# A decoder kernel: queries and keys written to DRAM as they are, and stacks gathered from them by many small DMAs

## The chip, the cores and the metric

The kernel runs on one core of a Trainium2 chip. A core has a matrix engine (TensorE, PE in the profile), a vector engine (VectorE, DVE), a scalar engine (ScalarE, ACT), GpSimd (POOL), and SyncE (SP), whose queue issues nearly all of this kernel's DMAs. Sixteen DMA engines move the data between DRAM and the on-chip memory of 128 partitions. The metric is the time of one execution on the device in microseconds (us), the median of several runs; lower is better.

## The reference

Input is x of shape 32 x 128 x 128 (batch, position, feature) and a context of the same shape. Two decoder layers follow each other, each part followed by a residual sum and a layer norm. Layer 0: an RWKV mixer, a block with self-attention, cross-attention and a feed-forward net, and a mixture of eight experts. Layer 1: a self-attention with rotary positions, a cross-attention, and a mixture of experts with capacity. The change touches the two attentions of layer 1. Both have 16 heads of dimension 8:

```
q = split_heads(x @ Wq + bq); k = split_heads(x @ Wk + bk); v = split_heads(x @ Wv + bv)
q = _rope(q); k = _rope(k)                                  # self-attention only
scores = einsum('bhqd,bhkd->bhqk', q, k) / sqrt(8)
probs  = softmax(scores)                                    # self-attention
attn   = silu(where(mask == 0, -1e9, scores * 8**-0.5))     # cross-attention, in place of the softmax
out    = einsum('bhqk,bhkd->bhqd', probs or attn, v) ... @ Wo
```

## The kernel before, in words

The 32 sequences are worked in eight groups of four (G = 4, GT = 512 columns). Each layer part is cut into units, eight for a group, and `place` puts the steps of a unit at unit numbers: the self-attention's steps by the table L6, the cross-attention's by L7. `pipeline` sorts all steps by that number and calls them in order, so that steps of neighbouring groups and parts lie between each other; a scheduler then fixes each engine's instruction order by priority and readiness. On the chip every engine runs its own list in order and waits on semaphores. SP's list is such a list too: a DMA that waits for something holds up all DMAs behind it.

In both attentions of layer 1 the score products have only 8 rows for each head. To use the matrix engine's rows, and to keep nearly float32 accuracy with bfloat16 products, a query or key is split into three bfloat16 parts (`parts3`, on POOL, four instructions each for q and k, lines 739 to 742). A score is the sum of six products of such parts, and the six blocks of 8 rows lie one under another in a "stack": row blocks 0 to 2 hold part pairs (q1,k3), (q2,k2), (q3,k1), blocks 3 and 4 the pairs (q1,k2), (q2,k1), block 5 the pair (q1,k1). The stack's two planes z = 0 and z = 1 hold q and k. Even heads use partitions 0 to 63, odd heads 64 to 127; a stack covers two of the four sequences (256 of the 512 columns).

[...] `spill` (lines 763 to 766) writes the parts into a scratch tensor `d_st` that already has the stack's row order; a part that stands in several products is written several times: one DMA of 768 KB and three of 256 KB. Rows 48 to 63 of each half come from a constant, written at the start into each of three scratch tensors (line 750): zeros, and ones in two rows of plane 1. `stack` (line 777) then reads a stack with two DMAs of 512 KB, one for each half of the partitions, in 512-byte pieces. `take(h)` calls it for columns half h = 0 and 1. Stacks lie in buffers with the tag `big` (five buffers, shared with other uses), or, for h = 0 of the self-attention from the third group on, in a weight buffer `w8`.

In the self-attention a first round of products (`cross(j, 0)`) serves only to find each row's maximum (`smax`, line 903). `mrow` turns the maxima, `mwrite` (line 916) writes them to DRAM in two bfloat16 parts, and `mread` (line 922) reads them into rows 48 and 49 of plane 0, opposite the ones, so that the second round (`cross(j, 1)`, then the exponential, line 930) subtracts the maximum inside the product. The cross-attention has no maximum and one round (`probs`, products added to a mask written by line 1060). A round is eight products of 64 rows each, pairwise on the two halves of the partitions, issued by `block` (lines 164 and 169).

Line 177 loads a group's x and line 186 stores it, line 514 loads the context and line 1022 the mask.

Of the kernel before, what the change touches and what calls it, by code (L numbers as in the profile page):

```python
# [11 lines left out]
BF = mybir.dt.bfloat16  # L12
# [11 lines left out]
GT = G * 128  # L24
# [45 lines left out]
class Net:  # L70
# [673 lines left out]
    def scratch(self, k):  # L744

        if self.dst is None:
            self.dst = []
            for i in range(3):
                d = self.dp.tile([64, 2, 8, 2, GT], BF, name=f"d_st{i}")
                self.nc.sync.dma_start(out=d[48:64], in_=self.a["pad_bf"])  # L750
                self.dst.append(d)
        return self.dst[k % 3]

    def parts(self):
# [2 lines left out]

    def spill(self, k, p):

        dma = self.nc.sync.dma_start  # L760
        d = self.scratch(k)
        rows = lambda lo, n: d[lo * 8:(lo + n) * 8].rearrange("(a d) r q z t -> (d r q) a z t", d=8)
        dma(out=rows(0, 3), in_=p)
        for z in range(2):
            dma(out=rows(3, 2)[:, :, z, :], in_=p[:, z:z + 2, z, :])
        dma(out=rows(5, 1)[:, 0], in_=p.rearrange("p a z t -> p (a z) t")[:, 0:6:5, :])
        return d

    def stack(self, d, h, slab=False):

        if slab:
            s = self.wp.tile([128, 4128], BF, name="w8", tag="w8", bufs=W8)
            s = s[:, 0:8 * GT].rearrange("p (q z t) -> p q z t", q=8, z=2)
        else:
            s = self.t("stack", [8, 2, GT // 2], BF)
        for par in range(2):
            self.nc.sync.dma_start(out=s[par * 64:par * 64 + 64], in_=d[:, par, :, :, h * 256:h * 256 + 256])
        return s

    def pad9(self):  # L780
# [61 lines left out]
    def att_units(self, g, getw, done):  # L842
        nc, sm = self.nc, self.sm
        w = Later(getw)
        st = {}
# [28 lines left out]
            st["d"] = self.spill(g, st.pop("p"))  # L874

        def take(h):
            st["s", h] = self.stack(st["d"], h, g > 1 and h == 0)

        def vproj(b):
            st["v", b] = self.v9proj(g, b, st["xh"], st["xl"], w["w"][0][:, 512:640], w["w"][1][:, 512:640], w["bv"])  # L880
# [1 line left out]
        def cross(j, l):  # L882

            b, pq = j // 2, j % 2
            t = slice(b % 2 * 128, b % 2 * 128 + 128)
            sk = st["s", b // 2]
            s = [self.pst("cross1" if l else "cross0") for _ in range(2)]
            calls = []
            for k in range(4):
                for par in range(2):  # L890
                    p = slice(par * 64, par * 64 + 64)
                    calls.append((s[par][:, k * 128:(k + 1) * 128], sk[p, pq * 4 + k, l, t],
                                  sk[p, pq * 4 + k, 1 - l, t], dict(start=True, stop=True)))
            self.block(calls)
            return s
# [76 lines left out]
        for j in range(8):  # L972
            h, odd = j // 4, j % 2
# [36 lines left out]
    def xat_units(self, g, getw, done):  # L1010
        nc = self.nc
        w = Later(getw)
        st = {}
# [41 lines left out]
        def probs(j):  # L1055
            b, pq = j // 2, j % 2
            t = slice(b % 2 * 128, b % 2 * 128 + 128)
            s = [self.pst("silu1" if j % 2 else "silu0") for _ in range(2)]
            for par in range(2):
                nc.tensor.matmul(out=s[par], lhsT=self.identb,  # L1060
                                 rhs=st["m"][:, b, :].unsqueeze(1).to_broadcast([128, 4, 128]), start=True, stop=False)
            calls = []
            for k in range(4):
                for par in range(2):
                    r = slice(par * 64, par * 64 + 64)
                    calls.append((s[par][:, k * 128:(k + 1) * 128], st["s", b // 2][r, pq * 4 + k, 1, t],
                                  st["s", b // 2][r, pq * 4 + k, 0, t], dict(start=False, stop=k == 3)))
            self.block(calls)
            ps = []
            for par in range(2):  # L1070
                p = self.t("xp")
                nc.scalar.activation(p, s[par], AF.Tanh, scale=0.5 * 8 ** -0.5)
                st["last", j] = nc.vector.scalar_tensor_tensor(p, p, 1.0, s[par], ALU.add, ALU.mult)
                ps.append(p)
            st["p", j] = ps
# [377 lines left out]
def prep(i):  # L1453
    c = np.ascontiguousarray
    f = np.float32
    pairs = lambda w: c(w.reshape(8, 128, 128).transpose(1, 0, 2).reshape(128, 1024))
    d = {
        "xtok": c(i["x"].transpose(1, 0, 2)),
        "xT": c(i["x"].transpose(2, 0, 1).reshape(128, 4096)),
        "ctxT": c(i["ctx_1024"].transpose(2, 0, 1).reshape(128, 4096)),  # L1460
        "mask0": c(i["mask_BxS2_bk0"].reshape(4096)),
        "rwkv_w": c(np.concatenate([i["L0_attn_" + n].T for n in ("Wk", "Wv", "Wr", "Wo")], axis=1)),
        "rwkv_v": c(np.stack([i["L0_attn_" + n] for n in
                              ("mix_k", "mix_v", "mix_r", "spatial_decay", "spatial_first")], axis=1)),
    }
    for n in ("sa", "ca"):
        for k in ("wq", "wk", "wv"):
            d[f"{n}_{k}"] = c(i[f"L0_xattn_{n}_{k}"])
        d[f"{n}_wo"] = pairs(i[f"L0_xattn_{n}_wo"])
        d[f"{n}_bo"] = c(i[f"L0_xattn_{n}_bo"])  # L1470
    for n in ("ln1_g", "ln1_b", "ln2_g", "ln2_b", "ln3_g", "ln3_b"):
        d[n] = c(i["L0_xattn_" + n])
    d["fc1_w"] = c(i["L0_xattn_fc1_w"])
    d["fc2_w"] = c(i["L0_xattn_fc2_w"].reshape(4, 128, 128).transpose(1, 0, 2).reshape(128, 512))
    d["fc1_b"] = c(i["L0_xattn_fc1_b"].reshape(4, 128).T)
    d["fc2_b"] = c(i["L0_xattn_fc2_b"])

    d["moe_w1"] = c(i["L0_ffn_w1"].transpose(2, 0, 1).reshape(128, 2048))
    d["moe_w2"] = c(i["L0_ffn_w2"].reshape(8, 128, 2, 128).transpose(3, 0, 2, 1).reshape(128, 2048))
    d["moe_b1"] = c(i["L0_ffn_b1"].reshape(16, 128).T)  # L1480
    d["moe_b2"] = c(i["L0_ffn_b2"])
    d["moe_nw"] = c(i["L0_ffn_norm_weight"].reshape(128, 1))
    d["moe_gate"] = c(i["L0_ffn_gate_w"].T)
    order = np.array([(2 * q + r) * 8 + k for k in range(8) for r in range(2) for q in range(8)])
    partner = np.array([o + 4 if o % 8 < 4 else o - 4 for o in order])
    w = [i["L1_attn_Wq"], i["L1_attn_Wk"]]
    d["a1_w"] = c(np.concatenate([w[0][:, order], w[0][:, partner], w[1][:, order], w[1][:, partner],
                                  i["L1_attn_Wv"]], axis=1))
    b = [i["L1_attn_bq"], i["L1_attn_bk"]]
    d["a1_b"] = c(np.stack([b[0][order], b[0][partner], b[1][order], b[1][partner]], axis=1))  # L1490
    d["a1_bv"] = c(i["L1_attn_bv"])
    d["a1_bo"] = c(i["L1_attn_bo"])
    heads = np.array([2 * (pq * 4 + k) + par for pq in range(2) for par in range(2) for k in range(4)])
    rows = (heads[:, None] * 8 + np.arange(8)).reshape(128)
    d["a1_wo"] = c(i["L1_attn_Wo"][rows])
    inv = (np.float32(1.0) / np.power(np.float32(10000.0), np.arange(0, 8, 2, dtype=f) / np.float32(8))).astype(f)
    ang = np.arange(128, dtype=f)[None, :] * inv[order % 4][:, None]
    d["a1_cos"] = c(np.cos(ang).astype(f))
    d["a1_sin"] = c((np.sin(ang) * np.where(order % 8 < 4, -1, 1).astype(f)[:, None]).astype(f))
    import ml_dtypes  # L1500
    pad = np.zeros((16, 2, 8, 2, GT), ml_dtypes.bfloat16)
    pad[:2, :, :, 1] = 1
    d["pad_bf"] = pad
    d["x1_w"] = c(np.concatenate([i["L1_xattn_Wq"].T[:, order], i["L1_xattn_Wk"].T[:, order], i["L1_xattn_Wv"].T], axis=1))
    d["x1_b"] = c(np.stack([i["L1_xattn_bq"][order], i["L1_xattn_bk"][order]], axis=1))
    d["x1_bv"] = c(i["L1_xattn_bv"])
    wo = np.zeros((4, 4, 32, 128), f)
    wo[:, :, :8] = i["L1_xattn_Wo"].T[rows].reshape(4, 4, 8, 128)
    d["x1_wo"] = c(wo.reshape(4, 128, 128).transpose(1, 0, 2).reshape(128, 512))
    d["mask1"] = c(i["mask_Bx1xSxS2_ik1"][:, 0].transpose(2, 0, 1))  # L1510
    d["m1_gate"] = c(i["L1_ffn_gate_w"].T)
    w1, w3, w2 = (i["L1_ffn_" + n] for n in ("w1", "w3", "w2"))

    d["m1_w13"] = c(np.concatenate([w1[:, :, :384], w1[:, :, 384:], w3[:, :, 384:], w3[:, :, :384]], axis=2)
                    .transpose(1, 0, 2).reshape(128, 8 * 896))
    w2p = np.zeros((8, 512, 128), f)
    w2p[:, :448] = w2
    d["m1_w2"] = c(w2p.reshape(8, 4, 128, 128).transpose(2, 0, 1, 3).reshape(128, 4096))
    d["tri"] = np.triu(np.ones((128, 128))).astype(ml_dtypes.bfloat16)
    return d  # L1520
# [16 lines left out]
```

## Time and profile before

| | us |
|---|---|
| three runs | 1865.32, 1872.02, 1865.08 |
| median | 1865.32 |
| the profiled execution | 1872.84 |
| its span, first to last instruction | 1871.1 |
| layer 1's attentions, first spill to last stack issued | 1125.8 to 1572.1 |
| PE busy, of 1240 to 1390 | 127.20 |
| PE busy, of 1390 to 1600 | 179.54 |

The profile is of one execution. Its page gives busy time by engine, then forty equal slices of the span (46.8 us each) in which a digit is the busy share in tenths, PEclk the clock that the matrix engine was granted, DMA the mean busy share of the sixteen DMA engines and GB/s what they moved. Other views give waits (who waited for whom, total time, times, longest), a timeline of one queue, the chain of work that ended last, and any of them for a window of time. A line number is that of the kernel; where a helper records an instruction, it is the helper's.

### The profile page before, as it was taken

The numbers are of one execution on the slowest core, as the hardware profiler recorded it, in microseconds if no ns is written. First come the engines' busy times: TensorE is split into PE (matmuls) and PEld (weight loads), VectorE is DVE, ScalarE is ACT, GpSimd is POOL, SyncE is SP. The second block draws the span as 40 slices with busy tenths as digits, with TensorE's granted clock in tenths as the row PEclk, the third lists the DMA queues.
The fourth block names the chain that finished last, engine by engine and source line by source line (L and its number), as shares of the span: only waits on it lengthen the run. The fifth ranks groups of instructions, "written<-read, shape, count | busy, mean of one in ns | idle before, by whom it ended". The sixth has DMA issues, their size and how long they took to land.

```text
span 1871.1 us, 44846 instructions
## 1 busy us (share of the span) xinstructions
PE 1728.4 (92%) x15658; PEld 1400.8 (75%) x15658; DVE 1383.4 (74%) x5256; ACT 1177.4 (63%) x3703; POOL 863.3 (46%) x1201
## 2 busy tenths in 40 slices
PE   5899999989999999999999999999779888898998
PEld 3677777777778788887788888866556555688888
DVE  7978888776766676666776677677655767789896
ACT  2776766768777777777645554346666646556654
POOL 4655555564544444444434444245432432246555
PEclk7999999999999999999999999999998989899999
DMA  5101101010110000100133435468979988222222
GB/s 158 36 31 40 39 20 41 31 53 26 48 48 26 20 13 25 42 8 12 57 119 123 164 134 130 109 179 198 200 191 225 217 197 205 73 81 92 96 90 70
DMA packets 148770, 171.45 MB, mean 92 GB/s; under 512 B 13128, under 2 KB 100176, under 8 KB 146064
## 3 DMA queue, kind: packets, MB, share of 16 engines
q1 hardware_dynamic: 145808, 154.95, 31.0%
q0 software_dynamic: 1584, 11.54, 1.5%
q8 instruction: 124, 2.03, 0.5%
q10 hardware_dynamic: 1152, 2.10, 0.3%
q14 instruction: 102, 0.84, 0.1%
HBM read 114.81 MB, written 55.31 MB: 91 GB/s over the span
## 4 chain that ended last, share of the span: by engine, by line
PE 62%; DVE 18%; ACT 6%; DMA 5%; POOL 4%; issue 3%; SPq 1%; POOLq 0%; ACTq 0%; DVEq 0%
PE mm L489 6%; PE S L705 6%; PE mm L152 6%; PE mm L153 5%; PE mm L154 5%; PE PV L169 4%; PE PT L452 4%; PE S L169 3%; DVE e L432 3%; PE PV L164 3%; PE PT L1283 3%; ACT e L437 2%; DMA x<-x 2%; PE S L164 2%; PE S L554 2%
## 5 line engine op out<-in xcount | busy, mean ns | idle before, releaser
L437 ACT ACTIVATE e<-e,nm 128x128 f32<-128x128 f32 x1024 | 397.6, 391 | 108.5 <-POOL nm L434 106.4
L441 POOL TENSOR_TENSOR e<-e,ri 128x512 f32<-128x512 f32 x256 | 266.1, 1044 | 205.0 <-DVE ri L439 185.7
L432 DVE CUSTOM_DVE_ANT_0 e<-S,msk 128x128 f32<-128x128 f32 x1024 | 228.7, 284 | 21.5 <-PE PT L452 12.8
L437 ACT ACTIVATION_READ_ACCUMULATOR e<-e,nm 128x1 f32 x1024 | 193.1, 189 | 0.0
L452 PE MATMUL PT<-ident,e 128*128 128x128 f32 x1024 | 150.8, 278 | 6.8 <-ACT v L397 4.6
L169 PE MATMUL S<-qk 64*128 64x128 f32 x1792 | 148.5, 280 | 0.0
L169 PE MATMUL PV<-pt,v 128*64 128x128 f32 x1792 | 141.1, 277 | 0.0
L452 PEld LDWEIGHTS PT<-ident,e 128*128 128x128 f32 x1024 | 115.6, 141 | 32.7 <-issue 8.7
L694 ACT ACTIVATE v<-mm,col_moe_b 128x512 f32<-128x512 f32 x128 | 85.5, 685 | 81.8 <-PE mm L154 81.3
L705 PEld LDWEIGHTS S<-w,v 128*128 128x128 f32 x1024 | 128.6, 191 | 7.8
L705 PE MATMUL S<-w,v 128*128 128x128 f32 x1024 | 133.7, 276 | 0.0
L152 PE MATMUL mm<-xs,w 128*128 128x512 f32 x296 | 127.2, 441 | 4.7 <-DVE qk L409 1.9
L489 PE MATMUL mm<-w,big 128*128 128x128 f32 x1024 | 127.6, 278 | 0.0
L489 PEld LDWEIGHTS mm<-w,big 128*128 128x128 f32 x1024 | 120.9, 192 | 7.6 <-issue 5.0
L439 DVE RECIPROCAL ri<-su 128x4 f32<-128x4 f32 x256 | 43.4, 173 | 110.7 <-ACT e L437 106.4
L169 PEld LDWEIGHTS S<-qk 64*128 64x128 f32 x1792 | 123.9, 188 | 0.4 <-DVE x L220 0.4
L153 PE MATMUL mm<-xs,w 128*128 128x512 f32 x296 | 118.9, 402 | 1.6 <-DVE xs L146 1.6
L434 POOL TENSOR_SCALAR nm<-mx 128x4 f32<-128x4 f32 x256 | 58.6, 233 | 133.1 <-DVE mx L432 119.5
L154 PE MATMUL mm<-xs,w 128*128 128x512 f32 x296 | 118.4, 400 | 0.0
L230 POOL TENSOR_SCALAR rsqv<-bmv 128x4 f32<-128x4 f32 (+1 forms) x73 | 14.4, 197 | 214.4 <-DVE bmv L203 197.7
L454 ACT COPY pt<-PT 128x512 f32<-128x512 f32 x128 | 74.3, 581 | 59.5 <-PE PT L452 58.8
L169 PEld LDWEIGHTS PV<-pt,v 128*64 128x64 f32 x1792 | 108.7, 137 | 2.3 <-issue 2.2
(324 smaller groups left out, 5052.1 us busy)
## 6 DMA issues: line engine op xcount, KB each, us to landing
x<-x SPq DMA_DIRECT2D x151, 256.0 KB
big<-d_st SPq DMA_DIRECT2D x52, 512.0 KB
pt<-d_w SPq DMA_DIRECT2D x64, 256.0 KB
d_st<-qk SPq DMA_DIRECT2D x48, 256.0 KB
d_st<-qk SPq DMA_DIRECT2D x16, 768.0 KB
d_w<-big POOLq DMA_DIRECT2D x11, 1024.0 KB, 5.1
w<-d_w SPq DMA_DIRECT2D x7, 1024.0 KB
w<-d_st SPq DMA_DIRECT2D x12, 512.0 KB
```

Source lines behind the costliest of these rows:

```text
L152: mm(out=out, lhsT=wh, rhs=xh, start=True, stop=False)
L153: mm(out=out, lhsT=wh, rhs=xl, start=False, stop=False)
L154: mm(out=out, lhsT=wl, rhs=xh, start=False, stop=True)
L164: i = mm(out=out, lhsT=w, rhs=x, **more)
L169: i = mm(out=out, lhsT=w, rhs=x, **more)
L432: self.seen = nc.vector.tensor_tensor_reduce(e[:, t], s[h][:, t], msk[:, t], 1.0, NEG, ALU.add, ALU.max, mx[:, b:b + 1])
L437: nc.scalar.activation(e[:, t], e[:, t], AF.Exp, bias=nm[:, b:b + 1], scale=0.125, accum_out=su[:, b:b + 1])
L441: nc.gpsimd.tensor_tensor(e3, e3, ri.unsqueeze(2).to_broadcast([128, G, 128]), ALU.mult)
L452: nc.tensor.transpose(pt[:, t], es[h][:, t], self.ident)
L489: nc.tensor.matmul(out=o[:, b, :], lhsT=st["ot", p // 4][:, p % 4, b * 128:(b + 1) * 128], rhs=w["wo"][:, p * 128:(p + 1) * 128], start=p ...
L694: nc.scalar.activation(h, hp, AF.Gelu, bias=w["b1"][:, k:k + 1])
L705: nc.tensor.matmul(out=o[:, b, :], lhsT=hs[i][:, b * 128:(b + 1) * 128], rhs=w["w2"][:, k * 128:k * 128 + 128], start=i == 0, stop=i == 1)
```

## The change

The parts are written to DRAM once, as they are: `spill` is two DMAs of 384 KB, one for each half of the columns, into a scratch tensor of 128 rows, 2 halves, 6 (part and plane) and 256 columns. `stack` gathers each block of 8 rows by its own DMA: three (blocks 0 to 2) in pieces of 1 KB, since there both planes lie side by side, and three (blocks 3 to 5) in pieces of 512 bytes. That is twelve DMAs of 64 KB for a stack tile where there were two of 512 KB; the self-attention has two more, which bring two rows of ones. The padding rows are no longer read, and the products go over 48 rows (50 in the second round of the self-attention). The order of the projections' output features changes on the host to suit (`order`: the half of the heads is now the outermost index), and the three constant writes at the start go.

```diff
     def scratch(self, k):
         if self.dst is None:
-            self.dst = []
-            for i in range(3):
-                d = self.dp.tile([64, 2, 8, 2, GT], BF, name=f"d_st{i}")
-                self.nc.sync.dma_start(out=d[48:64], in_=self.a["pad_bf"])
-                self.dst.append(d)
+            self.dst = [self.dp.tile([128, 2, 6, GT // 2], BF, name=f"d_st{i}") for i in range(3)]
         return self.dst[k % 3]

     def spill(self, k, p):
+        d = self.scratch(k)
+        pv = p.rearrange("f a z (h t) -> f h (a z) t", h=2)
+        for h in range(2):
+            self.nc.sync.dma_start(out=d[:, h], in_=pv[:, h])
+        return d
+
+    def stack(self, d, h, ones=False, slab=False):
         dma = self.nc.sync.dma_start
-        d = self.scratch(k)
-        rows = lambda lo, n: d[lo * 8:(lo + n) * 8].rearrange("(a d) r q z t -> (d r q) a z t", d=8)
-        dma(out=rows(0, 3), in_=p)
-        for z in range(2):
-            dma(out=rows(3, 2)[:, :, z, :], in_=p[:, z:z + 2, z, :])
-        dma(out=rows(5, 1)[:, 0], in_=p.rearrange("p a z t -> p (a z) t")[:, 0:6:5, :])
-        return d
-
-    def stack(self, d, h, slab=False):
         if slab:
             ...
         else:
             s = self.t("stack", [8, 2, GT // 2], BF)
+        v = d.rearrange("(r d q) h c t -> r h d q c t", d=8, r=2)
         for par in range(2):
-            self.nc.sync.dma_start(out=s[par * 64:par * 64 + 64], in_=d[:, par, :, :, h * 256:h * 256 + 256])
+            rows = lambda k, n=1: s[par * 64 + k * 8:par * 64 + (k + n) * 8]
+            src = v[par, h]
+            for k in range(3):
+                dma(out=rows(k).rearrange("d q z t -> d q (z t)"),
+                    in_=src[:, :, 2 * k:2 * k + 2].rearrange("d q z t -> d q (z t)"))
+            for k, c in ((3, slice(0, 4, 3)), (4, slice(2, 6, 3)), (5, slice(0, 6, 5))):
+                dma(out=rows(k), in_=src[:, :, c])
+            if ones:
+                dma(out=s[par * 64 + 48:par * 64 + 50, :, 1], in_=self.a["pad_bf"][0:2, par, :, 1, 0:256])
         return s
 ...
         def take(h):
-            st["s", h] = self.stack(st["d"], h, g > 1 and h == 0)
+            st["s", h] = self.stack(st["d"], h, True, g > 1 and h == 0)
 ...
-                    p = slice(par * 64, par * 64 + 64)
+                    p = slice(par * 64, par * 64 + 48 + 2 * l)
 ...
-                    r = slice(par * 64, par * 64 + 64)
+                    r = slice(par * 64, par * 64 + 48)
 ...
-    order = np.array([(2 * q + r) * 8 + k for k in range(8) for r in range(2) for q in range(8)])
+    order = np.array([(2 * q + r) * 8 + k for r in range(2) for k in range(8) for q in range(8)])
```

## The prediction

> **What bounds the kernel now.** I read the page's slices first: only slices 25 to 34 (1120 to 1590 us, layer 1's two attentions) have busy DMA engines.
>
> ```profile
> span 1871.1 us, 44846 instructions
> ...
> PE   5899999989999999999999999999779888898998
> ...
> PEclk7999999999999999999999999999998989899999
> DMA  5101101010110000100133435468979988222222
> GB/s 158 36 31 40 39 20 41 31 53 26 48 48 26 20 13 25 42 8 12 57 119 123 164 134 130 109 179 198 200 191 225 217 197 205 73 81 92 96 90 70
> ```
>
> Elsewhere PE is full and no scratch transfer matters. Here PE falls to 7 or 8, its clock dips, and DMA reaches 8 and 9 at only about 200 GB/s. Next, who queues: the SP queue in order of time (start, duration, line), one group of the self-attention.
>
> ```profile
> 1258.55 0.58 SPq L777 DMA_DIRECT2D w<-d_st  x1
> 1259.24 0.79 SPq L922 DMA_DIRECT2D big<-d_m  x2
> 1260.07 0.58 SPq L777 DMA_DIRECT2D w<-d_st  x1
> 1260.70 2.98 SPq L777 DMA_DIRECT2D big<-d_st  x2
> 1263.73 2.72 SPq L765 DMA_DIRECT2D d_st<-qk  x1
> 1266.48 0.58 SPq L916 DMA_DIRECT2D d_m<-m  x1
> 1274.23 0.90 SPq L922 DMA_DIRECT2D w<-d_m  x2
> 1275.23 0.55 SPq L766 DMA_DIRECT2D d_st<-qk  x1
> 1275.88 0.89 SPq L765 DMA_DIRECT2D d_st<-qk  x1
> 1276.87 0.45 SPq L763 DMA_DIRECT2D d_st<-qk  x1
> ...
> 1281.82 0.58 SPq L777 DMA_DIRECT2D w<-d_st  x1
> ```
>
> This is a closed loop of 23.3 us (1258.55 to 1281.82) in which SP idles only for landings: four stack loads, the write of the row maxima behind them (landed at 1274.2), its reading back, the spill, its landing, the next stacks. The waits of that queue from 1240 to 1600 us (total, times, longest) say the same:
>
> ```profile
> SPq L922 <- DMA d_m<-m: 45.0, 8, 8.7
> SPq L777 <- DMA d_st<-qk: 41.6, 17, 6.2
> ```
>
> The DMA view of 1389 to 1408 us (40 columns of 0.475 us) shows how fast the stacks go.
>
> ```profile
> DMA  2956989799999999999999999999999999999960
> GB/s 70 177 138 259 517 310 466 332 289 272 181 179 172 180 213 202 182 177 173 182 212 199 179 177 175 183 213 197 181 174 196 250 385 404 410 397 358 367 203 13
> ...
> big<-d_st SPq DMA_DIRECT2D x4, 512.0 KB
> ```
>
> The engines are busy throughout, but while the stacks go (each writes 64 partitions) they move about 180 GB/s; the loads behind them, which write 128 partitions, go at 385 to 410. At each change from one half of the partitions to the other the rate rises to 213. Packet size alone is not it: the last stores of the output, also 512-byte packets, reach 288 GB/s. So the stacks' rate goes with the partitions they write, some 2.9 GB/s for each. Last, the chain from 1385 to 1600 us:
>
> ```profile
> 1385.86 4.34 DMA d_st<-qk
> 1390.29 6.47 DMA big<-d_st
> ...
> 1474.23 7.41 DMA x<-x
> 1496.17 7.76 DMA x<-x
> ```
>
> The cross-attention's first stack is waited for outright, later the x loads that queue behind stacks (five pieces, 33.8 us).
>
> **The change part by part.**
>
> *The spill.* Four DMAs of 1.5 MB in all become two of 384 KB. SP issues 2 at about 0.6 (row L766, 0.55, plus a gap) instead of 0.55, 0.89 and 0.45 at the loop's end: -0.9 us. In exchange both need all eight POOL steps of the parts, where L765 and L766 could leave early. SP stood waiting on POOL for the parts in either form; nothing behind them leaves sooner or later by more than an issue. The last part's landing was 3.4 to 4.3 us on the chain for the 768 KB DMA; 768 KB in 512-byte packets at the output stores' 288 GB/s last 2.7 us, plus the 2.0 us an empty transfer takes below, 4.7. That is +0.4; I take the spill as -0.5 a group.
>
> *The stacks.* Two DMAs of 512 KB for each take become 12 (cross-attention) or 14 (self-attention). Of a pair of takes, 24 are row blocks of 64 KB that write eight partitions each; the four of ones are 8 KB. Bytes read a group fall from 2 to 1.5 MB. What one block costs is the unknown.
> - Lower end: SP's issue. The one DMA of eight partitions in the trace (moe_b, 4 KB) takes 0.38 us to issue and the next starts 0.42 us after it; the 256 KB loads issue at 0.32 to 0.43. So 0.44 us a block, and about 2.0 us to the landing of such a small one (moe_b: 1.99).
> - Upper end: if eight partitions get the 2.9 GB/s each that they get now, 64 KB take 2.8 us, as every block is alone.
> - Between: blocks of one stack go to different partitions, so what overlaps wins back rate. SP's issues carry eight landing semaphores in turn, so at most eight are in flight, but they start in order and meet on the same partitions. The ends' geometric mean is 1.1 us; as some overlap is certain, I take 0.95.
>
> [...]
>
> *Self-attention.* At 0.95 us, 24 blocks last 22.8 us; with 2.0 us to land and 0.4 for the ones the last stack is there after 25.2 us, against 13.7 now (issued from 1258.55, its semaphore full at 1272.3). The write of the maxima stands behind it on SP and its engines. The loop becomes 23.3 + 11.5 - 0.5 = 34.3 us, +11 a group. The first three groups are spaced 34 to 41 us by the expert layer's work and can hold this. Five loops (1258.6 to 1367, groups 3 to 7) are tight: +55. Against it stand 5 us that the last group's stacks still arrive before the first use (landed 1358.4, used 1363.3): 50.
>
> *Cross-attention.* Its first stack (12 blocks) lands after 11.4 + 2.0 = 13.4 us instead of 9.3: +4. Later groups: the last block is issued at about 24 x 0.95 - 8 x 0.95 + 1.5 = 16.7 us, the x loads and the spill by 19, and they land behind the blocks and each other near 22.8 + 2 + 4.5 = 29.3; the loop now takes 25.5 (1390.3 to 1568.9, seven times). +3.8 x 7 = 26.
>
> *The PE side.* The products have 48 or 50 rows instead of 64; a product's time (212 to 216 ns for 128 columns) goes with columns; nothing. A first use now waits on up to eight landing semaphores instead of two; one such wait in PE's queue lasts 51 ns, so 32 x 6 x 51 ns = 10 us at most. Where PE is idle anyway it is free; I take 0, and 10 for the upper end.
>
> *The three pad DMAs* at 31 us go: SP gets 1.8 us back, before work that waits for DVE. Nothing.
>
> Sum: 50 + 4 + 26 = +80. The profiled execution took 1872.84 us (span 1871.1); it would be 1953. The median of the runs, 1865.32, lies 7.5 below, so 1945.
>
> **The rivals.**
> 1. *Faster: the blocks flow at SP's pace.* If a block costs 0.44 us, the last stack lands after 10.6 + 2.0 = 12.6 us, -1.1, and the spill gives -0.5 to -1: some 2 us for each of 12 loops, 25, of which PE's own work (it is busy for over 92% of five of the twelve loops) leaves 15: 1850. For it: a quarter to a half less data, and the first 1 us of a stack does run at 281 GB/s. Against: the steady 180. It decides below about 0.5 us a block: 24 x 0.49 + 2 = 13.7.
> 2. *Half the engines, no other limit.* If a block's packets go to half of the engines and each takes the stacks' present 49 ns (mean of the packet records from 1240 to 1560 us), a stack has 576 packets, 72 an engine instead of 64: 3.5 us, a pair of takes 14.1 + 2: +2.4 x 5 = 12, the cross-attention within its slack, so 1877; with part of PE's waits 1882. It ends on the slow side too, or unmeasurably.
> 3. *Little overlap.* Blocks at 1.6 us (midway, in ratio, between 0.95 and 2.8): 38.4 + 2.4 us a pair, +26.6 x 5 - 5 in the self-attention, +12 at the first and +19.4 x 7 in the cross-attention: 2140. For it: in-order starts, equal sizes. Against: the rate does rise when neighbours go to different partitions (213).
> 4. *The change does less than it says*: the bytes do fall, 12.6 MB fewer written and 8.4 fewer read; this only fails to matter. It is in rival 2.
>
> **How the numbers follow.** Forecast (0.7 to 1.2 us a block, which the same sum turns into 1886 to 2021 us): 0.46. Rival 1: 0.27. Rival 2: 0.17. Rival 3: 0.10. Under 0.5% (9 us) a measurement of this kernel tells nothing from no change. Of rival 1, 0.23 are faster and 0.04 the same; of rival 2, 0.04 the same. Faster 0.23, same 0.08, slower 0.69. The range leaves out the faster part of rival 1 and most of rival 3: 1845 to 2040.
>
> **What would show it.** DMA time: the rate between a pair's first issue and its last landing falls to some 60 GB/s, and the stretch grows from 13.7 to about 25 us. The SP loops of the self-attention read 33 to 35 us. PE's share and clock in slices 27 to 34 fall further (clock 0.64 to 0.88 in loops where PE idles now). The waits of the first products for the stacks, 5.1 us in all now, grow to tens. Wrong, if blocks are issued every 0.44 us and land within 3 us of issue; then SP's order alone decides and it is rival 1.

## The result

The changed kernel takes 1944.5 us (median of four runs, 1936.8 to 1947.1), the kernel before 1867.0 (1865.1 to 1872.0) beside it: a ratio of 1.0405, 95% interval 1.0383 to 1.0428, slower. The forecast was 1945.0, slower. That the number fits to half a microsecond is partly luck. The profiled execution of the changed kernel took 1936.81 us, the fastest of its four, and that of before 1872.84, slower than its four: between those two traces lie 64 us, not 78. What the traces can explain is the 64, and the prediction's own terms miss parts of it in both directions.

The head of the page of the changed kernel, its slices:

```profile
span 1934.7 us, 45277 instructions
...
PE   5899999999999999999999998877757979798998
...
PEclk7999999999999999999999999889877989799999
DMA  4111110111100000001244433355557766232222
GB/s 121 35 38 32 35 41 19 41 45 47 46 25 19 25 25 25 29 12 56 84 140 149 150 82 69 80 139 113 105 153 135 133 148 185 65 98 88 88 90 75
```

PE now falls below 9 from slice 25 on (1161 us), where before it did so from slice 29 on (slice 9 apart), and its clock falls to 7 and 8 where it was 8 and 9. Over the span the granted clock is 0.952 where it was 0.970, and PE is busy for 1742.2 us where it was 1728.4, with the same 15658 products; how much of these 14 us lies on the path was not tried. The DMA engines are *less* busy than before (5 to 7 tenths in slices 27 to 34, where 6 to 9 stood) and move less, 105 to 185 GB/s for 179 to 225. So the transfers became slower without the 16 engines becoming full. That is the first clue.

The SP queue in order of time, one group of the self-attention (start, duration, line):

```profile
1300.17 2.07 SPq L776 DMA_DIRECT2D w<-d_st  x3
1302.35 0.68 SPq L926 DMA_DIRECT2D big<-d_m  x2
1303.07 2.57 SPq L779 DMA_DIRECT2D w<-d_st  x3
...
1310.01 0.66 SPq L776 DMA_DIRECT2D big<-d_st  x1
1310.77 0.39 SPq L920 DMA_DIRECT2D d_m<-m  x1
1311.21 1.35 SPq L776 DMA_DIRECT2D big<-d_st  x2
1314.74 0.54 SPq L926 DMA_DIRECT2D w<-d_m  x2
1315.32 2.17 SPq L779 DMA_DIRECT2D big<-d_st  x3
...
1327.28 2.07 SPq L776 DMA_DIRECT2D w<-d_st  x3
```

Three blocks take 2.07 us: 0.66 us of issue each and 0.04 between them, whether the block's source is two adjacent parts (L776) or two separate ones (L779). A loop is now 27.1 us (1300.17 to 1327.28), not the 34.3 forecast. The write of the row maxima (L920) and their reading back (L926) do not stand behind the last block: they are issued between blocks. The waits of that queue from 1240 to 1640 us (total, times, longest) confirm it: both waits that filled the old loop shrank, from 45.0 and 41.6 us.

```profile
SPq L926 <- DMA d_m<-m: 27.6, 10, 6.3
SPq L776 <- DMA d_st<-qk: 21.3, 10, 5.5
```

The DMA view of 1188 to 1202 us (40 columns of 0.35 us), where the blocks of the second group go almost alone:

```profile
DMA  4539567676665565565576676666655565655675
GB/s 105 88 56 138 48 82 59 50 86 50 54 92 53 53 94 50 64 88 47 67 75 51 78 60 50 81 57 50 91 53 56 85 61 56 94 50 51 85 59 60
...
big<-d_st SPq DMA_DIRECT2D x17, 64.0 KB
```

Seventeen blocks are issued there, the engines are 5 to 7 tenths busy, and 68 GB/s pass (the view's mean): 64 KB in 0.96 us. The view sums the time of the queue's packets to 60.4% of sixteen engines; for the old stacks (1147 to 1158 us), where nearly all digits are 9, the packets overlap and sum to 113%, so this is about half. In a usual loop of the self-attention there is more room still, 47.1% from 1300 to 1322 us. Over all 16 groups the blocks land 0.91 us apart and 4.5 us after their issue in the mean, so about five are under way at a time. Landings are counted on eight semaphores in turn; a stack DMA of 64 partitions posts 16 landing events, each of the 384 blocks 8 after a first one.

Last, the chain by line between the first take (1139) and 1272 us, where the expert layer still runs. Before, in the same window:

```profile
by line: PE S L705 28.7%; PE mm L152 11.6%; PE mm L154 10.4%; PE mm L153 10.4%; DVE amx L903 3.2%; DMA res<-in_ctxT_dram 2.8%; PE mm L169 2.7%; PE S L554 2.7%; issue 2.7%; PE PT L191 2.5%; PE PT L714 2.4%; DMA x<-x 2.1%; ACT e L930 1.9%; PE
```

After:

```profile
by line: DMA big<-d_st 13.7%; PE S L705 12.4%; SPq L779 8.0%; SPq L776 7.9%; PE mm L152 6.6%; PE mm L153 5.3%; DMA x<-x 5.2%; PE mm L154 5.1%; DMA d_st<-qk 4.2%; DMA xb<-in_mask_dram 3.9%; issue 3.3%; DMA d_m<-m 2.5%; POOL pt L869 1.9%; PE 
```

Before, that stretch belonged to PE and no stack was on the chain at all. Now 30% of it are blocks, waited for in transfer or in issue. A part of that chain in time:

```profile
1193.68 7.14 DMA big<-d_st
...
1200.84 6.82 DMA big<-d_st
...
1207.72 5.22 DMA xb<-in_mask_dram
...
1212.96 0.07 DVE msk L1030
```

A block issued at 1193.68 lands at 1200.82. The eighth transfer after it, which waits for the same landing semaphore, is issued at 1200.84; that one lands at 1207.66, and at 1207.72 the next in its turn is issued, which is the load of the cross-attention's mask. VectorE stands waiting for it (9.9 us) and PE behind VectorE.

Cut at the first stack load of each group, the two spans (1871.1 and 1934.7 us) differ like this, in us:

| stretch | before | after | change | forecast |
|---|---|---|---|---|
| to the first take | 1145.7 | 1139.0 | -6.7 | 0 |
| groups 0 to 3 (under the expert layer) | 112.9 | 133.1 | +20.2 | 0 |
| self-attention, groups 3 to 8 | 131.7 | 159.5 | +27.8 | +54 |
| cross-attention, 8 to the last take | 178.6 | 197.1 | +18.5 | +26 |
| last take to the end | 302.2 | 306.0 | +3.8 | 0 |

The self-attention's row is four loops of about +5.0 (90.3 to 110.2 us) and the passage to the cross-attention, 41.4 to 49.3. The chain by line from 1250 to 1640 us, where the attentions run, before and after:

```profile
by line: DMA x<-x 8.7%; PE PV L164 7.4%; PE PV L169 6.0%; PE PT L1086 5.5%; issue 4.3%; ACT e L930 3.8%; PE mm L152 3.6%; DVE e L1073 3.3%; PE S L169 3.0%; PE mm L1060 2.9%; PE S L1060 2.8%; PE mm L154 2.4%; DMA d_m<-m 2.3%; PE mm L153 2.3%
```

```profile
by line: DMA d_st<-qk 7.0%; PE PV L164 6.3%; SPq L776 6.0%; DMA big<-d_st 5.8%; issue 5.5%; SPq L779 5.4%; PE PV L169 5.0%; ACT e L934 4.1%; DMA x<-x 4.1%; DMA w<-d_w 3.3%; PE S L169 2.9%; PE PT L1090 2.7%; DMA d_m<-m 2.5%; PE mm L152 2.3%;
```

Before, the x loads stood first; now the spill's landing (7.0%) and the blocks in issue and transfer (17.2%) do, which together were under 5%.

### The profile page after: what moved, and what is told of

Read it like the earlier page. It is cut to its first block, busy times and chain, and to the rows that moved or that the text cites. A ratio compares the mean times of both kernels' runs of the same rounds, so it can differ in the third digit from the quotient of the medians.

```text
span 1934.7 us, 45277 instructions
## 1 busy us (share of the span) xinstructions
PE 1742.2 (90%) x15658; PEld 1409.9 (73%) x15658; DVE 1383.2 (71%) x5256; ACT 1178.6 (61%) x3703; POOL 862.8 (45%) x1201
## 3 DMA queue, kind: packets, MB, share of 16 engines
q10 hardware_dynamic: 1152, 2.10, 0.3%
## 4 chain that ended last, share of the span: by engine, by line
PE 54%; DVE 19%; DMA 8%; ACT 5%; POOL 5%; SPq 4%; issue 4%; ACTq 0%; POOLq 0%; DVEq 0%
PE mm L489 6%; PE mm L152 5%; PE S L705 4%; PE mm L153 4%; PE mm L154 4%; PE PV L169 4%; PE PT L452 3%; DVE e L432 3%; PE S L169 3%; PE PV L164 3%; PE PT L1287 2%; DMA big<-d_st 2%; ACT e L437 2%; PE S L164 2%; SPq L779 2%
## 5 line engine op out<-in xcount | busy, mean ns | idle before, releaser
L907 DVE TENSOR_REDUCE amx<-mm 128x4 f32<-128x512 f32 x128 | 82.5, 682 | 46.6 <-PE mm L169 46.0
L813 ACT COPY v<-PV 128x256 f32<-128x256 f32 x128 | 47.9, 374 | 105.9 <-PE PV L169 88.1
```

## The experiments

Two causes could make a block cost 0.9 us. The *queue theory*: SP needs 0.70 us to issue one, so their number decides. The *narrow theory*: a transfer of eight partitions is slow in itself. The prediction had put 0.44 us for the first and 2.8 for the second and taken 0.95 between them. Stretches below always lie between the first stack loads of groups, in one profiled execution of each kernel; the changed kernel's four executions lie 10 us apart, so a few us in a stretch say little.

**Cut by heads: as many DMAs, but wide.** In the kernel before, each stack DMA becomes seven of 64 partitions.

```diff
-            self.nc.sync.dma_start(out=s[par * 64:par * 64 + 64], in_=d[:, par, :, :, h * 256:h * 256 + 256])
+            for lo, hi in ((0, 2), (2, 3), (3, 4), (4, 5), (5, 6), (6, 7), (7, 8)):
+                self.nc.sync.dma_start(out=s[par * 64:par * 64 + 64, lo:hi], in_=d[:, par, lo:hi, :, h * 256:h * 256 + 256])
```

> The kernel before, with each of its 512 KB stack DMAs cut into seven by head (q): every piece still writes 64 partitions, 28 stack DMAs a group as in the changed self-attention; bytes, spill and products stay. Queue theory (the number of DMAs that SP has to issue, 0.66 us each and 0.04 between, is what the change costs): 28 issues last 19 us where four took 5, so the loops of the self-attention grow from 23 to 27 or 28 us and the time goes to 1920 to 1950 us. Narrow theory (blocks that write eight partitions are slow, whatever their number): pieces of 64 partitions still move 2 MB in 12.5 us at about 180 GB/s, the time stays below 1885 us.

Measured: 1908.6 us, ratio 1.0216 (1.0188 to 1.0243), between the two ranges, so both causes have a share. Half of the pieces land within 2.5 us of their issue, so transfer is hardly a limit; SP's pace is (13 issues of one take in SP's queue, seen from 1297 us on, and the chain from 1250 to 1640 us by line):

```profile
1296.50 8.87 SPq L778 DMA_DIRECT2D big<-d_st  x13
```

```profile
by line: SPq L778 19.5%; DMA big<-d_st 6.7%; DMA w<-d_w 5.8%; issue 5.0%; PE PT L1087 4.4%; PE PV L164 4.1%; PE PV L169 3.4%; DVE e L1074 3.2%; DMA d_st<-qk 2.6%; DMA res<-in_ctxT_dram 2.6%; DVE amx L904 2.5%; DMA x<-x 2.5%; DVE x L217 2.4%
```

28 issues at 0.65 us a group cost about 2%. The four loops of the self-attention last 111.9 us here, as long as with the changed kernel's narrow blocks (110.2; 90.3 before): there the number of issues is enough. The first three groups stay at 114.4 us, though a pair of takes lasts 22.4 to 26.5 us, as in the changed kernel, which needs 133.1: under the expert layer the issues are hidden so long as the transfers land promptly, which points to the narrow blocks for the loss there. The cross-attention is longer than the changed kernel's (209.7 against 197.1 us); why was not tried.

**Cut by rows: the same number, narrow.** In the kernel before, each stack DMA becomes six of eight partitions and one of 16.

```diff
+            for lo, hi in ((0, 8), (8, 16), (16, 24), (24, 32), (32, 40), (40, 48), (48, 64)):
+                self.nc.sync.dma_start(out=s[par * 64 + lo:par * 64 + hi], in_=d[lo:hi, par, :, :, h * 256:h * 256 + 256])
```

> The kernel before, with each of its 512 KB stack DMAs cut into seven by rows: six blocks of eight partitions (64 KB each) and one of sixteen (the padding, 128 KB); 28 DMAs a group, the same bytes, the same spill. Queue theory: the same time as the cut by head, 1920 to 1950 us, since the number of issues is the same. Narrow theory: slower than the cut by head by 20 us or more, 1940 to 1990 us, and blocks land about 1 us apart.

Measured: 1947.5 us, 1.0434 (1.0404 to 1.0463). The narrow theory's side: over 20 us slower than the wide cut, though these blocks take only 0.27 to 0.32 us to issue. But its takes lie spread around its spill (26 to 51 us a pair; see the cut with halves in turn), so how much of the 39 us between the two cuts is width is not shown. The DMA view of 1147 to 1156 us, blocks alone:

```profile
DMA  9656666666666666666656666666666997685656
GB/s 159 75 91 91 87 80 100 80 84 93 93 84 91 93 89 89 96 93 87 102 87 96 102 96 91 102 98 100 98 100 102 191 221 87 39 41 27 30 36 61
```

92 GB/s in the middle, 0.71 us a block where about 1 was expected, and six tenths busy; the moment the 16-partition pieces go (the 9s) the share is full. Transfers are waiting and the share stays at six tenths; in the changed kernel's trace a block of the same eight partitions posts eight landing events, where a stack DMA of 64 posts 16. Both fit blocks that use only about half of the engines.

**Halves in turn, changed kernel.** The blocks of the two halves alternate.

```diff
-        for par in range(2):
-            ...
+        for k in range(3):
+            for par in range(2):
+                dma(out=rows(par, k).rearrange("d q z t -> d q (z t)"),
+                    in_=v[par, h][:, :, 2 * k:2 * k + 2].rearrange("d q z t -> d q (z t)"))
+        ...
```

> The changed kernel with only the order of a stack's DMAs changed: block by block, the half of the partitions 0 to 63 and the half 64 to 127 in turn, so that neighbouring DMAs write different halves. The number of DMAs and the bytes stay. Narrow theory: neighbours no longer meet on the same partitions, blocks land 0.70 us apart in every group (now 0.77 to 1.09), and the time falls by 20 us or more, to 1900 to 1925 us. Queue theory: SP issues at the same pace, 1935 to 1950 us.

Measured: 1940.3 us, 1.0383 (1.0359 to 1.0407): the intervals of this and of the changed kernel (1.0383 to 1.0428) overlap, so no gain can be claimed; the time is in the queue theory's range. In its second group the blocks do land sooner, 3.4 to 5.2 us after their issue instead of up to 8.1. Over all 16 groups nothing moved: blocks land 0.92 us apart in the mean instead of 0.91, and a pair of takes is there after 25.1 us instead of 24.9. Which half the neighbour writes does not set this kernel's pace.

**Halves in turn, cheap issue.** The same in the cut by rows, where a block takes 0.27 to 0.32 us to issue: do neighbours in the queue hold each other up when they write the same half?

```diff
-        for par in range(2):
-            for lo, hi in ((0, 8), ... (48, 64)):
+        for lo, hi in ((0, 8), ... (48, 64)):
+            for par in range(2):
```

> The kernel before, its stacks cut by rows as in the earlier run (six blocks of 8 partitions and one of 16 to each half, issue 0.27 us), with the two halves taken in turn block by block. [...]

Measured: 1944.6 us, 1.0411 (1.0386 to 1.0437); the interval overlaps that of the cut by rows (1.0404 to 1.0463), so no gain can be claimed. But its view of 1148 to 1157 us shows that the rate did change:

```profile
DMA  6656666666666666666566666666666666699999
GB/s 100 107 121 112 114 130 105 128 125 109 132 100 134 118 114 130 107 137 112 116 130 107 143 98 130 121 123 132 100 137 112 125 125 107 148 271 246 153 112 114
```

About 120 GB/s instead of 92, which fits neighbouring partitions getting in each other's way (the order of the source changed with it); the share is still six tenths. What holds the blocks at 120 was not shown. That the time did not follow probably comes from this kernel's spill in four parts (argued, not tried): the takes are spread around the spill, and the queue of SP waits from 1240 to 1640 us in many small pieces and for more spills.

```profile
SPq L778 <- DMA d_st<-qk: 62.3, 32, 5.7
...
SPq L778 <- DMA big<-d_st: 30.1, 79, 1.4
```

So the two row cuts do not give a clean price for a block, only rates.

**Cut by 16 rows.** Four DMAs of 128 KB to a half, in the kernel before.

```diff
+            for lo in range(0, 64, 16):
+                self.nc.sync.dma_start(out=s[par * 64 + lo:par * 64 + lo + 16], in_=d[lo:lo + 16, par, :, :, h * 256:h * 256 + 256])
```

> The kernel before, each 512 KB stack DMA cut by rows into four of 16 partitions and 128 KB with 16 engines each: 16 DMAs a group instead of 4. Narrow theory: a transfer of 16 partitions alone gets a quarter of the 180 GB/s, but several are in flight; if blocks of eight partitions pay 0.68 us for 64 KB, 128 KB on 16 pays 0.8 to 1.3 us, a pair of takes 13 to 21 us, 1880 to 1915 us. Queue theory: 16 issues of 0.31 us are 5 us a group, as now, no change: 1860 to 1875 us.

Measured: 1920.7 us, 1.0263 (1.0226 to 1.0300), on the narrow theory's side and a little beyond its range (here, too, the takes lie spread around the spill). View of 1142 to 1152 us:

```profile
DMA  9999999999999999999999999999999999999999
GB/s 125 104 100 117 125 119 104 98 129 123 109 111 100 127 121 111 98 125 186 104 98 92 121 125 100 94 119 141 119 104 94 145 119 107 109 117 137 119 100 98
```

All engines are busy, and 115 GB/s pass (the view's mean), 1.14 us for 128 KB. Here the engines are not short. The same packets go at 290 GB/s when 128 partitions are written (below), which leaves the partitions.

**48 rows.** The kernel before without the 16 pad rows; the ones get DMAs of their own.

```diff
-            self.nc.sync.dma_start(out=s[par * 64:par * 64 + 64], in_=d[:, par, :, :, h * 256:h * 256 + 256])
+            self.nc.sync.dma_start(out=s[par * 64:par * 64 + 48], in_=d[:, par, :, :, h * 256:h * 256 + 256])
+            if ones:
+                self.nc.sync.dma_start(out=s[par * 64 + 48:par * 64 + 50, :, 1], in_=self.a["pad_bf"][0:2, par, :, 1, 0:256])
```

> The kernel before without the padding: stacks of 48 rows a half instead of 64 (384 KB instead of 512), products over 48 or 50 rows, and in the self-attention the two rows of ones by an own small DMA, as in the changed kernel; spill and wide stack DMAs stay as before. If the bytes set the stacks' pace (packets at 49 ns), a pair of takes lands after 9.5 instead of 12.5 us and the time falls to 1835 to 1858 us. [...]

Measured: 1864.8 us, 0.9989 (0.9972 to 1.0006): nothing. A quarter of the stacks' bytes is gone, and the stacks still land 12 to 15 us after the first issue: 150 GB/s (the mean from 1146 to 1153 us) for 48 partitions instead of 188 (the mean from 1147 to 1158 us before) for 64. The bytes that the change saves are worth nothing here.

**One DMA of 128 partitions.** The other direction: in the kernel before, the scratch gets the two halves as its outer axis, and a take is one DMA of 1 MB. The spill needs eight DMAs for its four.

```diff
-                d = self.dp.tile([64, 2, 8, 2, GT], BF, name=f"d_st{i}")
+                d = self.dp.tile([2, 64, 8, 2, GT], BF, name=f"d_st{i}")
...
-        for par in range(2):
-            self.nc.sync.dma_start(out=s[par * 64:par * 64 + 64], in_=d[:, par, :, :, h * 256:h * 256 + 256])
+        self.nc.sync.dma_start(out=s, in_=d.rearrange("r p q z t -> (r p) q z t")[:, :, :, h * 256:h * 256 + 256])
...
-    order = np.array([(2 * q + r) * 8 + k for k in range(8) for r in range(2) for q in range(8)])
+    order = np.array([(2 * q + r) * 8 + k for r in range(2) for k in range(8) for q in range(8)])
```

> The kernel before, with the two r halves as the outer axis of the scratch, so that a take is ONE DMA of 1 MB that writes all 128 partitions with 16 engines; the spill becomes 8 DMAs of 64 source partitions instead of 4 of 128. Partition theory (a transfer's rate goes with the partitions that are written at one time): the 1 MB goes at 380 to 410 GB/s as the other 128-partition loads do, 2.7 us a take instead of 5.4 to 5.8, the two stacks of a group land 8 to 9 us after their first issue instead of 13.7; the self-attention loops (23.3 us) then lose up to 5 us each, the kernel ends at 1825 to 1850 us. Byte theory (the stacks' rate is that of 512-byte packets or of DRAM, whatever the partitions): landing stays at 13 to 14 us, and the four more spill issues (0.4 to 0.5 us each, two loops in three feel them) make 1865 to 1885 us.

Measured: 1851.1 us, 0.9904 (0.9885 to 0.9922): faster than both kernels, a microsecond outside the range. View of 1147 to 1154 us:

```profile
DMA  4798999999999999999999999999999999999873
GB/s 140 173 219 231 269 293 339 348 345 345 348 424 304 287 295 290 287 298 284 263 243 281 298 310 284 293 322 310 301 307 304 290 293 298 293 269 234 211 184 91
```

290 to 300 GB/s where 180 passed, and two stacks land 9.8 to 12.8 us after the first issue instead of 12.7 to 15.4. That is the partition theory, with a smaller gain than it had: the 380 to 410 of the other loads are not reached. The rate is that of the output's last stores, which have the same 512-byte packets (288 GB/s); that the packets set it was not tried. Self-attention 131.7 to 126.1 us, cross-attention 178.6 to 158.4.

**Two queues.** In the changed kernel ACT's queue issues the blocks of the upper half.

```diff
+            dma = self.nc.scalar.dma_start if par else self.nc.sync.dma_start
```

> The kernel after, with the blocks of the lower 64 partitions issued by SP as now and those of the upper 64 issued by ACT's queue. Queue theory (0.70 us of issue per block on one queue is what sets the pace): SP issues only half, both halves flow at once, the blocks of a pair of takes land within 12 to 16 us of the first issue; the kernel gets back 20 to 40 us of the 78, 1905 to 1925 us, unless ACT (which also does exp and copies) is held up by its 14 issues of 0.66 us a group, about 9 us a group: then 1925 to 1960. Narrow theory (eight partitions a block, what the DMA side can take): the blocks land no faster than every 0.8 us, the last 22 us or more after the first issue, 1930 to 1960 us.

Measured: 1931.0 us, 1.0348 (1.0323 to 1.0374): some 10 us back of 78 by the ratio. The chain around 1290 us says why not more:

```profile
1287.99 5.14 DMA w<-d_st
1293.15 0.67 ACTq L780
1293.86 0.60 ACT e L935
1294.46 0.33 ACTq L780
1294.88 5.19 DMA big<-d_st
1300.09 0.67 ACTq L780
```

A block lands, which lets ACT issue the next, and ACT's exponential (L935) stands behind that issue. The eight landing semaphores go round over both queues (in the trace of before, ACT's store of x issued at 1276.85 us already counts on one of SP's eight), so a second queue adds no transfers in flight. An issue lasts 0.66 us where a block lands every 0.91; what the second queue saved was still small: a pair of takes is there after 22.0 us in the mean instead of 24.9.

**Fewer blocks.** In the changed kernel one DMA of 24 partitions fills the rows of the last three blocks of a half, from other rows of the scratch: 16 row DMAs a group instead of 24.

```diff
-            for k, c in ((3, slice(0, 4, 3)), (4, slice(2, 6, 3)), (5, slice(0, 6, 5))):
-                dma(out=rows(k), in_=src[:, :, c])
+            flat = d.rearrange("p h c t -> (p h c) t").rearrange("(n m two) t -> n m two t", m=16, two=2)
+            dma(out=rows(3, 3).rearrange("p q z t -> p (q z) t"), in_=flat[par * 24:par * 24 + 24, :, h])
```

> The kernel after, with the three last blocks of each half (24 rows, 192 KB) filled by one DMA of the same size and packet size from other rows of the scratch: this leaves out the right contents of rows 24 to 47 of each half, the time alone is read. [...] Queue theory (0.70 us of issue a block): 8 issues fewer, 5.6 us, and the blocks stay on SP's pace: the last stack lands 17 to 20 us after the first issue; the twelve tight loops and the first three give back 3 to 5.6 us each, 1885 to 1915 us. Narrow theory (the engines and partitions of 8-row blocks alone set the pace): 12 blocks of 0.7 to 0.9 us and 4 of 24 rows at some 130 GB/s (1.5 us) make 15 to 17 us, 1880 to 1905 us; a result above 1925 speaks against both, and for something that the number of DMAs and their width do not touch.

Measured: 1913.5 us, 1.0253 (1.0230 to 1.0276); the stacks land 16.7 to 22 us after the first issue. That is in the queue theory's range and 8.5 us above the narrow one's; the pairs' landing (19.6 us in the mean) is in the queue theory's 17 to 20 too and not in the other's 15 to 17. It speaks for the issues, weakly, since the narrow theory's price was an estimate. The first three groups are back at 114.0 us: there a pair lands after 18.6 to 20.0 us where the changed kernel needs 22.4 to 26.5.

**What the first three groups wait for.** Four loads (three x loads and the mask) are moved from SP's queue to ACT's, in the changed kernel.

```diff
-            st["x"] = self.getx(g)
+            st["x"] = self.getx(g, nc.scalar)
...
-            nc.sync.dma_start(out=st["mi"], in_=self.a["mask1"][:, g * G:(g + 1) * G, :])
+            nc.scalar.dma_start(out=st["mi"], in_=self.a["mask1"][:, g * G:(g + 1) * G, :])
```

> The kernel after, with the expert layer's x load, the self-attention's second x load, the cross-attention's x load and its mask load issued from ACT's queue instead of SP's, where they stand behind up to 28 block issues (20 us). If the first three groups lose their 20 us (112.9 to 133.1 us between the first and the fourth take) because those loads come late, they fall back to 113 to 122 us and the kernel to 1920 to 1935 us. If it is the stacks themselves, or the write and read of the row maxima, which stay on SP, that come late, nothing is regained: 1940 to 1950 us; where ACT now waits for these loads' buffers, 1950 to 1965.

Measured: 1940.5 us, 1.0409 (1.0352 to 1.0465), and 136.7 us for the three groups (in the slowest of its four executions): nothing. But it was no test of late loads, since they stayed late. The chain:

```profile
1208.65 7.41 DMA big<-d_st
...
1216.09 0.04 ACTq L1026
...
1216.16 6.60 DMA xb<-in_mask_dram
```

The mask load, now on ACT's queue, starts when a block lands that SP issued 7.4 us earlier, eight transfers before: same turn, other queue. As a control, the same edit in the version with one DMA of 128 partitions:

> The wide-scratch version (one 1 MB stack DMA of 128 partitions to a take), with the same four loads issued from ACT's queue. There SP issues two stack DMAs a group in 3 us, so the loads are not late: within 0.5% of the wide version, 1842 to 1860 us. Faster than 1840 would say that SP's order holds up even that kernel; over 1860, that ACT's waits for these loads' buffers cost more than SP's.

1842.6 us, 0.9884 (0.9853 to 0.9916 is nearly the interval of that version without it, 0.9885 to 0.9922): about the same, perhaps a little better, and the lowest median of the study.

So the mask load was taken away altogether; the mask is a constant.

```diff
-            st["mi"] = self.t("mi", [G, 128], I32)
-            nc.sync.dma_start(out=st["mi"], in_=self.a["mask1"][:, g * G:(g + 1) * G, :])
...
-            nc.vector.tensor_scalar(st["m"], st.pop("mi"), 0.0, -1e9, ALU.is_equal, ALU.mult)
+            nc.vector.memset(st["m"], 0.0)
```

> The kernel after without the cross-attention's mask loads: the mask is a constant written by VectorE, which leaves the mask's content out of the computation, so only the time is read. Shared-turn theory (in the first three groups the price is paid by the first thing that VectorE needs from a transfer issued behind the blocks, the mask load; eight transfers in flight, handed out over all queues, keep it back until the last blocks have landed): the first three groups fall from 133 us to 115 to 125 us, the kernel to 1925 to 1938 us, and VectorE's 9.9 us wait for the mask is gone. Stack theory (the stacks themselves, or the row maxima, are late there): something else behind the blocks takes the mask's place on the chain, 130 to 135 us for the three groups, 1938 to 1948 us.

Measured: the second group falls from 49.0 to 38.9 us (38.2 before the change), and its chain is PE's again from end to end, until an x load:

```profile
1202.59 1.56 PE S L705 x14
...
1206.94 1.61 PE S L705 x14
...
1211.10 4.10 DMA x<-x
```

The three groups take 125.6 us, just outside the range. In these two traces the mask load was the second group's whole price; the first group (48.5 us, 40.8 before the change) waits for an x load in the same way. The kernel, however, takes 1942.1 us, 1.0410 (1.0380 to 1.0440), the same ratio as the changed kernel's and not the 1925 to 1938 that the shared turn had forecast. Against the changed kernel's trace the first take comes 4.4 us later and the cross-attention takes 6.4 more; both are differences of single executions. So the wait for the mask is shown, and that the kernel is slower for it is not: what became of the 7.5 us that the three groups regained stays open.

## Why the prediction came out, point by point

- *The bottleneck* (SP's closed loop and the DMA rate by partitions) was right: 128 partitions at once bring 290 GB/s and 1% of the time, a quarter fewer bytes bring nothing. That many narrow transfers cost the 4%, and that the bytes saved win nothing, the runs show; how the 78 us divide between number and width they show for the self-attention's loops alone.
- *A block at 0.95 us* was right as a size, by luck: it was picked between two ends that both failed, for an overlap between partitions, and taking the halves in turn changed nothing. In the loops it is SP's issue, 0.70 us, and what else SP issues and waits for between blocks that make it. They land every 0.77 to 1.09 us, 0.91 in the mean of the 16 groups. A pair of takes is there 22.0 to 29.3 us after its first issue (25.2 forecast); that is 62 GB/s (1.57 MB in 25.3 us, a usual group).
- *Its lower end, 0.44 us, was wrong.* It came from a DMA of eight partitions with another pattern. The blocks issue in 0.66 + 0.04 us, so *rival 1* (faster, below 0.5 us) could not happen. The upper end's reason, no overlap, was wrong too: blocks land every 0.91 us though each is under way for 4.5.
- *Rival 2* had the mechanism half right. What was measured fits its half of the engines: a block posts eight landing events where a stack DMA of 64 partitions posts 16, and the packets' time sums to 60.4% of the sixteen engines where the old stacks' made 113%. But SP's issue binds first, and in the second group the blocks move only 68 GB/s, so 1877 was far off.
- *"The write of the maxima stands behind it"* is the step that failed in the self-attention: it goes out between blocks, the loop grows by about 5.0 us and not by 11. The last block does land as late as forecast, 25.7 us after the first issue in the loop shown, but SP no longer waits for it: its row of issues, with one wait for the maxima, takes 23.4 us up to the spill, and 3.7 us later the next take begins. The two waits that the old loop stood in, 86.6 us in all, were room that blocks could fill, and they fell to 48.9.
- *"The first three groups can hold this"* failed the other way: +20.2 us. The profile before showed why it was unsafe: the chain there was PE's, without slack of its own, and every load behind the blocks is on it as soon as it is late. How long the stacks take does not decide it alone: with wide pieces the pairs took as long as here and the groups lost 1.5 us.
- *Cross-attention:* +26 forecast for the loops, +18.5 measured (28.2 us a loop; 29.3 forecast); the +4 for its first stack is +7.9 of the passage. Right in kind.
- *The spill* was mis-sized. In the self-attention's loops 3.5 to 4.6 us pass from its first issue to the next take, 6.4 to 7.1 before: nearly -3 a loop where -0.5 was taken. Its landing, taken as 4.7 us, lasts 2.9 to 8.2 where the chain has it between 1250 and 1640 us, six times, 27.5 us in all (7.8 before).
- *PE's waits at 0* held: PE waits 0.7 us for stacks, and in the 48-row run products of 48 rows last as long as those of 64 before (216 to 234 ns against 220 to 242, the means by line). The engines' waits for stacks grew from 5.1 to 19.0 us, most of it ACT's, "tens" only by rounding.
- The terms' errors (-26 in the self-attention, -8 in the cross-attention loops, +20 early, and a few) bring +80 to the traces' +64; that the medians differ by 78 made the total look better than its parts.

## What to carry to other kernels

Before a transfer is cut, ask three things of the trace: how long one issue lasts in exactly this pattern, how many partitions each piece writes, and how many pieces may be in flight. Here the issue alone allowed a block every 0.70 us, the transfers of the second group one every 0.96, and bytes saved bought nothing. Where a wide transfer is possible, make it wide: turning two halves of 64 partitions into one of 128 gave 1%, with more DMAs in the spill.

And when a long row of transfers is put into a queue, look for what is issued after it, on any queue that shares its landing semaphores; the first victims here were not the stacks but x loads and a mask load that nobody had thought of.

## What was not expected of the hardware

- The issue of a stack piece on SP that nothing holds up lasts between 0.27 and 0.66 us and goes with the pattern: 0.27 to 0.32 for a block whose rows match on both sides, 0.32 for 48 partitions, 0.58 to 0.61 for pieces of 64 partitions, 0.66 where 64 source rows are spread to eight partitions by eight.
- Rates while stacks go, by what is written: 290 to 300 GB/s (128 partitions), 180 (64), 150 (48), 115 (pieces of 16), 92 (blocks of eight in order), 120 (the same with the halves in turn), 68 (the changed kernel's blocks, which also gather from scattered rows). Why the rates differ so was not shown. In the row cuts a block that starts alone is there after 2.4 to 3.1 us. No block of the changed kernel starts alone; its quickest is there after 3.1.
- Why the changed kernel's blocks go at 68 and the row cut's at 92 stays open; source order and packet size differ, and neither was varied alone. The 68 are those of the second group; where SP sets the pace, a usual pair passes 62.
